# An adaLN + low-rank-expert FFN on one core: which DMA queue carries the first loads, and when the first stores leave

## The chip, the cores and the metric

The kernel runs on one NeuronCore of a Trainium2 chip. The metric is device microseconds (us) from launch to end; lower is better. Three runs of the kernel before the change took 791.09, 791.59 and 792.16 us, median 791.59. One further execution was recorded by the hardware profiler, and all durations below come from it.

Engines are called as in the profile: PE is TensorE (matmuls), PEld its weight loads, DVE is VectorE, ACT ScalarE, POOL GpSimd, SP SyncE. DMAs are issued in three places here: by SP (queue q1 of the profile), by ACT (q10), and by POOL (q0, software descriptors). All three feed the same 16 DMA engines.

## The reference

```
def cond(x, condition, weights):              # weights (16, 64, 64), one 64x64 matrix per sample
    return einsum('bct,bcd->bdt', x, weights[condition])
def ffn(y, A, B, Wr):                         # 64 experts of rank 16, top 16 of 64 per token
    scores = y @ Wr.T
    top_vals, top_idx = top_k(scores, 16)
    G = zeros(N, 64).at[rows, top_idx].set(softmax(top_vals))
    h = einsum('nd,krd->nkr', y, A)
    return einsum('nkr,kdr->nd', h * G[:, :, None], B) * 2.0
out = x + ffn(cond(x))                        # x is (64, 64, 1024) float32
```

So there are two 4096 x 1024 x 1024 products in float32, with the experts' gates multiplied in between, a small per-sample 64 x 64 product, and a residual add.

## The kernel before, in words

Tokens are handled in 8 groups of 512 rows. Each group has an "h" product (x with A) and an "o" product (the gated h with B). Both are done by Strassen-Winograd recursion: seven block products p1 to p7 instead of eight, built from sums and differences of blocks. For group 0 there is one level of it (functions z_whole and o_whole; matmuls at L542, tiles h_x, h_y, h_w, o_x, o_y, o_w). From group 1 on there are two levels (matmuls at L505). The second level needs sums of quarters of A and B ("leaves"). DVE makes these while group 0 is computed; leaf_steps makes them in a staging tile and stores them to HBM at L413 as h_p_p and o_p_p, and later parents fetch them from there (L458). Staging tiles come from the pool bsum, which has five buffers; the first four leaves use the tiles hb instead, which are still unused then. A sixth staging tile from bsum can only be written when the store out of the first has landed.

The schedule is written out by hand: the program order of each engine is the order in which the Python code calls it, and hooks (at(n, "mid" / "late" / "end", ...)) hang work for the other engines on the n-th parent product. Group 0 runs p1, p2, p5, p6, p7, p4, p3 of h. After p2 come the router scores of group 0, scores_t (L179, tile st), which need all four quarters of x and the router weight wr_sb. turn, scores, route_top, exps, rest, scaled and gates then turn these into gates; gates is a PE transpose (L301, tile gp) in the middle of p4, and gated (L321, tile zp) follows it.

What loads what at the start:

- ACT's queue: the first quarter of x in two parts, its three other quarters (L100, 512 KB each), and wr_sb (L118, 256 KB).
- SP's queue: a11 in two parts, a21, a12, a22 (L106, 1088 KB each), then the four blocks of B (L922, 1024 KB each).
- POOL's queue: cond_b (L110, the sample's condition broadcast to 128 partitions), the gathers of the 64 x 64 matrices (L157), six leaf stores of A's blocks a11 and a21 (L413), the residual rows of group 0 (L735, 512 KB each), later leaf stores.

A queue's DMAs are issued in order, and at most eight of those issued by SP and ACT together are in flight: where a ninth is due, its issuer waits for an earlier one to land, as the waits of SP's queue for DMAs of x show. Ten matmuls of the identity (L147, tile idle) run on PE ahead of the first product.

Of the kernel before, what the change touches and what calls it, by code (L numbers as in the profile page):

```python
# [15 lines left out]
P = 128  # L16
# [13 lines left out]
def kernel(  # L30
# [26 lines left out]
    nc = tc.nc  # L57
    N, T = x.shape
    B = cond.shape[1]
# [29 lines left out]
    def sub(o, a, b):  # L89
        nc.vector.tensor_tensor(o, a, b, ALU.subtract)  # L90
# [4 lines left out]
    def load_x(g: int, i: int, j: int, queue=nc.sync, parts=1):  # L95

        t = xq[g, i, j] = xp.tile([P, CH, HN], F32, tag=f"x{i}{j}", name=f"x_{g}_{i}{j}")
        for k in range(parts):
            s = ts(k, CH // parts)
            queue.dma_start(t[:, s, :], x_t[g, i, j][:, s, :])  # L100

    def load_block(name, src, r, c, pool, parts=1):
        t = pool.tile(src.shape[2:], F32, name=name)
        for k in range(parts):
            s = ts(k, CH // parts)
            nc.sync.dma_start(t[:, s, :], src[r, c][:, s, :])  # L106
        return t

    cond_b = const.tile([P, B], I32)
    nc.gpsimd.dma_start(cond_b, cond.to_broadcast([P, B]))  # L110
    load_x(0, 0, 0, nc.scalar, 2)
    a11 = load_block("a11", a_t, 0, 0, apool, 2)
    load_x(0, 1, 0, nc.scalar)
    a21 = load_block("a21", a_t, 1, 0, apool)
    load_x(0, 0, 1, nc.scalar)
    load_x(0, 1, 1, nc.scalar)
    wr_sb = epool.tile([P, 2 * CH, K], F32, name="wr_sb")
    nc.scalar.dma_start(wr_sb, wr_t)  # L118
    a12 = load_block("a12", a_t, 0, 1, apool)
    a22 = load_block("a22", a_t, 1, 1, apool)  # L120

# [19 lines left out]

    ident = const.tile([P, P], F32)
    make_identity(nc, ident)

    idle = acc.tile([P, P], F32, tag="acc", name="idle")
    for _ in range(10):
# [6 lines left out]
    def gather(g: int):  # L153
# [12 lines left out]
    hb = {  # L166
        (i, j): blocks.tile([P, CH, HN], F32, name=f"hb{i}{j}") for i in range(2) for j in range(2)
    }
# [171 lines left out]
    def left_sums(l):  # L340
        l11, l12, l21, l22 = l[0, 0], l[1, 0], l[0, 1], l[1, 1]
        ops = {"p1": l11, "p2": l12, "p4": l22}

        def tile_of(p):
            ops[p] = extra.tile([P, CH, HN], F32, tag="ex", name=f"sum_{p}")
            return ops[p]

        def s3():
            sub(l21, l11, l21)
            ops["p7"] = l21  # L350

        def s2():
            sub(tile_of("p6"), l22, ops["p7"])

        def s1():
            add(tile_of("p5"), ops["p6"], l11)

        def s4():
            sub(tile_of("p3"), l12, ops["p6"])

        def s1_s2():
            add(tile_of("p5"), l21, l22)
            sub(tile_of("p6"), ops["p5"], l11)

        return ops, {"s1": s1, "s2": s2, "s3": s3, "s4": s4, "s1_s2": s1_s2}
# [15 lines left out]
    def quads(t, w):  # L381

        return [[t[:, 2 * i : 2 * i + 2, ts(j, w)] for j in range(2)] for i in range(2)]

    leaf_d = {}
# [6 lines left out]
        (q11, _), (q21, q22) = quads(b_t[r, c], HALF)  # L392
        leaf_d.update({("o", j, "p1"): q11, ("o", j, "p2"): q21, ("o", j, "p3"): q22})

    unused = list(hb.values())

    def leaf_steps(k, j, block, apart=None):


        (q11, q12), (q21, q22) = quads(block, WIDTH[k])  # L400
        made = {}
        def staged(name):
            if apart is not None and unused:
                t = unused.pop().rearrange("p c k -> p (c k)")
                return t[:, : 2 * WIDTH[k]].rearrange("p (c k) -> p c k", c=2)
            t = bsum.tile([P, 2 * (HALF + KC)], F32, tag="leaf", name=name)
            return t[:, : 2 * WIDTH[k]].rearrange("p (c k) -> p c k", c=2)

        def step(op_, p, a, b):
            def f():  # L410
                made[p] = staged(f"{k}s_{j}_{p}")
                op_(made[p], *(made[v] if isinstance(v, str) else v for v in (a, b)))
                nc.gpsimd.dma_start(leaf_d[k, j, p], made[p])  # L413

            return f

        if k == "o":
            return [
                step(sub, "p5", q12, q11),
                step(sub, "p6", q22, "p5"),  # L420
                step(sub, "p4", q21, "p6"),
                step(sub, "p7", q22, q12),
            ]
        stay.update({(k, j, "p1"): q11, (k, j, "p2"): q21, (k, j, "p3"): q22, (k, j, "p5"): q12})
        t1 = q12 if apart is None else apart.rearrange("p (c k) -> p c k", c=2)
        steps = [
            step(sub, "p7", q22, q12),
            lambda: sub(t1, q12, q11),
            step(sub, "p6", q22, t1),
            step(sub, "p4", q21, "p6"),  # L430
        ]
        return steps if apart is None else steps + [lambda: nc.scalar.copy(q12, t1)]
# [416 lines left out]
    def x_operands(st):  # L849
        l = {(i, j): xq[st["g"], i, j] for i in range(2) for j in range(2)}  # L850
        st["x_ops"], st["x_sums"] = left_sums(l)
# [4 lines left out]
    def sums(st, which, *steps):  # L856
        for s in steps:
            st[which][s]()
# [61 lines left out]
    steps_of(first_steps["p2"], 4)  # L920
    for t, r, c in ((b12, 0, 1), (b22, 1, 1), (b11, 0, 0), (b21, 1, 0)):
        nc.sync.dma_start(t, b_t[r, c])  # L922
    x_operands(st)
    sums(st, "x_sums", "s1_s2")
    a_sums(1)
# [166 lines left out]
```

## Time and profile before

| what | value |
|---|---|
| runs | 791.09, 791.59, 792.16 us (median 791.59) |
| profiled execution, its own time | 791.37 us |
| its span, first to last instruction | 789.6 us |
| mean granted TensorE clock | 0.993 |
| PE busy | 772.7 us (98%) |
| DVE busy | 623.9 us (79%) |
| ACT, POOL busy | 184.7 us (23%), 76.5 us (10%) |
| DMA | 208.50 MB, mean 264 GB/s |

The profile page gives totals. The timeline lists instructions in order with, in brackets, the idle time before them and what ended it. The waits view sums such idle time by waiter and releaser. The windows view gives busy time, granted clock (PEclk) and DMA rate for chosen stretches. The DMA view lists queues and, for each issue, the size and the time to landing. Times are from the start of the span.

### The profile page before, as it was taken

The page shows a single profiled execution, that of the slowest core. Times are in us where ns is not written, and L with a number is a line of the kernel's source. Part 1 is how long each engine was busy: PE and PEld are TensorE (multiplying, and loading weights), DVE is VectorE, ACT ScalarE, POOL GpSimd, SP SyncE. Part 2 cuts the span into 40 slices and gives each one's busy share as a digit, 9 for nine tenths or more (in the row PEclk, how much of TensorE's full clock was granted, in tenths as well). Part 3 has the DMA queues.
Part 4 walks back from the last instruction along what each step waited for, and adds up shares of the span by engine and source line. Part 5 has one row for each costly group of instructions (what it writes and reads, how often), then busy time and mean ns, then how long its engine had stood idle before and what let it go on. Part 6 is the DMA issues. An engine that isn't in the chain of part 4 may idle for free.

```text
span 789.6 us, 14668 instructions
## 1 busy us (share of the span) xinstructions
PE 772.7 (98%) x5348; PEld 612.7 (78%) x5348; DVE 623.9 (79%) x1310; ACT 184.7 (23%) x490; POOL 76.5 (10%) x109
## 2 busy tenths in 40 slices
PE   8799999999999999999999999999999999999996
PEld 5344447888888888887888888888888888888885
DVE  3877875678788877898788977889768897688985
ACT  1031001223222322222223222232222231222221
POOL 4425353000010020000200001000200000000000
PEclk9899999999999999999999999999999999999999
DMA  9958569555778948887688968789488893687995
GB/s 327 410 214 287 193 245 307 184 186 161 279 244 284 349 129 323 270 294 263 217 291 280 307 213 278 264 279 339 140 309 275 277 352 121 220 267 250 343 384 209
DMA packets 107223, 208.50 MB, mean 264 GB/s; under 512 B 11072, under 2 KB 27200, under 8 KB 106256
## 3 DMA queue, kind: packets, MB, share of 16 engines
q1 hardware_dynamic: 99056, 183.33, 68.3%
q0 software_dynamic: 7088, 21.62, 7.8%
q10 hardware_dynamic: 1008, 2.62, 0.8%
q8 instruction: 43, 0.70, 0.3%
q14 instruction: 28, 0.23, 0.1%
HBM read 174.41 MB, written 33.11 MB: 263 GB/s over the span
## 4 chain that ended last, share of the span: by engine, by line
PE 93%; DMA 3%; DVE 2%; issue 0%; ACT 0%; DVEq 0%
PE h_p_x L505 23%; PE o_p_x L505 20%; PE h_p_w L505 12%; PE o_p_w L505 10%; PE h_p_y L505 6%; PE o_p_y L505 5%; PE zp L321 4%; PE o_x L542 4%; DMA wr_sb<-in_wr_t_dram 3%; PE h_x L542 3%; PE o_w L542 2%; PE h_w L542 2%; PE sw L221 1%; PE gp L301 1%; DVE o L87 1%; PE o_y L542 1%
## 5 line engine op out<-in xcount | busy, mean ns | idle before, releaser
L505 PE MATMUL o_p_x<-lo_p_p,l_t 128*128 128x256 f32 x584 | 142.9, 379 | 0.0
L505 PEld LDWEIGHTS o_p_x<-lo_p_p,l_t 128*128 128x128 f32 x584 | 111.0, 190 | 15.4
L87 DVE TENSOR_TENSOR o<-o,m_o_p 128x1024 f32<-128x1024 f32 (+1 forms) x67 | 78.8, 1195 | 0.5
L157 POOL DMA_INDIRECT w_st<-in_cw_dram,idx x32 | 34.0, 1061 | 431.2 <-PE zp L321 413.4
L87 DVE TENSOR_TENSOR m_h_p<-h_p_w,l_a 128x272 f32<-128x272 f32 x49 | 21.5, 440 | 62.5 <-PE h_p_w L505 62.5
L87 DVE TENSOR_TENSOR m_h_p<-m_h_p,m_h_p 128x1088 f32<-128x1088 f32 x49 | 62.3, 1283 | 0.2
L505 PE MATMUL h_p_x<-a,l_t 128*128 128x272 f32 x224 | 60.5, 392 | 0.0
L505 PE MATMUL h_p_w<-lh_p_p,l_t 128*128 128x272 f32 x196 | 53.8, 397 | 0.0
L505 PE MATMUL h_p_x<-lh_p_p,l_t 128*128 128x272 f32 x196 | 52.9, 392 | 0.0
L505 PE MATMUL o_p_w<-lo_p_p,l_t 128*128 128x256 f32 x196 | 51.1, 383 | 0.0
L334 DVE TENSOR_TENSOR hb<-zp,gg 128x512 f32<-128x512 f32 x64 | 39.9, 684 | 12.0 <-PE zp L321 12.0
L505 PEld LDWEIGHTS h_p_x<-a,l_t 128*128 128x128 f32 x224 | 42.6, 190 | 8.6
L598 ACT COPY l_b<-h_p_x 128x272 f32<-128x272 f32 x49 | 18.9, 386 | 121.8 <-PE h_p_x L505 119.5
L505 PE MATMUL h_p_x<-at,l_t 128*128 128x272 f32 x168 | 45.4, 392 | 0.0
L505 PEld LDWEIGHTS h_p_x<-lh_p_p,l_t 128*128 128x128 f32 x196 | 37.2, 190 | 7.5
L598 ACT COPY l_b<-o_p_x 128x256 f32<-128x256 f32 x49 | 18.2, 372 | 103.8 <-PE o_p_x L505 103.8
L505 PEld LDWEIGHTS h_p_w<-lh_p_p,l_t 128*128 128x128 f32 x196 | 36.5, 191 | 7.0
L505 PEld LDWEIGHTS o_p_w<-lo_p_p,l_t 128*128 128x128 f32 x196 | 36.6, 190 | 5.2
L87 DVE TENSOR_TENSOR m_o_p<-o_p_w,l_a 128x256 f32<-128x256 f32 x48 | 20.3, 423 | 23.2 <-PE o_p_w L505 23.2
L321 PEld LDWEIGHTS zp<-w_st,m_h_p 64*64 64x64 f32 x2048 | 31.7, 135 | 7.9 <-issue 7.9
L505 PEld LDWEIGHTS h_p_x<-at,l_t 128*128 128x128 f32 x168 | 31.9, 190 | 6.6
L605 ACT COPY m_h_p<-h_p_x 128x272 f32<-128x272 f32 x49 | 18.9, 387 | 70.7 <-PE h_p_x L505 70.7
(173 smaller groups left out, 1393.4 us busy)
## 6 DMA issues: line engine op xcount, KB each, us to landing
lo_p_p<-o_p_p SPq DMA_DIRECT2D x280, 256.0 KB, 3.7
lh_p_p<-h_p_p SPq DMA_DIRECT2D x147, 272.0 KB, 5.6
lo_p_p<-in_b_t_dram SPq DMA_DIRECT2D x63, 256.0 KB, 4.1
x<-in_x_t_dram SPq DMA_DIRECT2D x28, 512.0 KB, 5.5
o<-in_x_dram SPq DMA_DIRECT2D x28, 512.0 KB, 7.0
out_dram<-o SPq DMA_DIRECT2D x27, 512.0 KB, 4.4
o_p_p<-os_p_p POOLq DMA_DIRECT2D x28, 256.0 KB, 3.3
h_p_p<-hs_p_p POOLq DMA_DIRECT2D x17, 272.0 KB, 2.8
```

Of the source, the lines that this page charges most:

```text
L87: nc.vector.tensor_tensor(o, a, b, ALU.add)
L157: nc.gpsimd.indirect_dma_start(out=w_st[:, i, :], out_offset=None, in_=cw, in_offset=bass.IndirectOffsetOnAxis(ap=idx[:, n : n + 1], axis=0),)
L221: nc.tensor.matmul(sw[r, i, ts(k, K // 2)].rearrange("p (d k) -> p d k", d=2), lhsT=ws[g][r, i, :], rhs=halves(st["z"][i // 2, k])[r, i % ...
L301: nc.tensor.transpose(gp[:, i, :], st["g2"][i].rearrange("p a k -> p (a k)"), ident)
L321: nc.tensor.matmul(zp[b][e * D : (e + 1) * D, c, s, :], lhsT=halves(z)[r, s, c // 2, ds(c % 2 * P + e * D, D)], rhs=ws[g][r, 2 * i + s, :] ...
L334: nc.vector.tensor_tensor(tokens(hb[j, i])[:, :, :, b, :], zp[b], g_ij[:, :, :, b, :], ALU.mult)
L505: nc.tensor.matmul(bank, lhsT=v[:, c, :], rhs=w[:, c, :width], start=first and c == 0, stop=c == 1, skip_group_check=True,)
L542: nc.tensor.matmul(piles[n, s], lhsT=left()[j][:, c, ts(s, P)], rhs=w, start=c == 0 and PILES[kind][j].isupper(), stop=c == CH - 1, skip_g ...
L598: nc.scalar.copy(par["val"][n], par["bank"]["x"])
L605: nc.scalar.copy(before["q"][0][1], before["bank"]["x"])
```

## The change

The three other quarters of x and wr_sb go from ACT's queue to SP's, where they stand between the blocks of A in the order in which the program uses them. The load of cond_b on POOL moves behind the two POOL instructions that make the identity. The six stores of the first leaves (those of a11 and a21) go from POOL's queue to SP's, behind the four loads of B; their staging tiles stay occupied until those stores have landed. No computation changes.

```
     cond_b = const.tile([P, B], I32)
-    nc.gpsimd.dma_start(cond_b, cond.to_broadcast([P, B]))
     load_x(0, 0, 0, nc.scalar, 2)
     a11 = load_block("a11", a_t, 0, 0, apool, 2)
-    load_x(0, 1, 0, nc.scalar)
+    load_x(0, 1, 0)
     a21 = load_block("a21", a_t, 1, 0, apool)
-    load_x(0, 0, 1, nc.scalar)
-    load_x(0, 1, 1, nc.scalar)
+    load_x(0, 0, 1)
+    load_x(0, 1, 1)
     wr_sb = epool.tile([P, 2 * CH, K], F32, name="wr_sb")
-    nc.scalar.dma_start(wr_sb, wr_t)
+    nc.sync.dma_start(wr_sb, wr_t)
     a12 = load_block("a12", a_t, 0, 1, apool)
     a22 = load_block("a22", a_t, 1, 1, apool)
...
     ident = const.tile([P, P], F32)
     make_identity(nc, ident)
+    nc.gpsimd.dma_start(cond_b, cond.to_broadcast([P, B]))
...
-    unused = list(hb.values())
+    unused, to_store = list(hb.values()), []
...
                 op_(made[p], *(made[v] if isinstance(v, str) else v for v in (a, b)))
-                nc.gpsimd.dma_start(leaf_d[k, j, p], made[p])
+                if apart is None:
+                    nc.gpsimd.dma_start(leaf_d[k, j, p], made[p])
+                else:
+                    to_store.append((leaf_d[k, j, p], made[p]))
...
     for t, r, c in ((b12, 0, 1), (b22, 1, 1), (b11, 0, 0), (b21, 1, 0)):
         nc.sync.dma_start(t, b_t[r, c])
+    for d, t in to_store:
+        nc.sync.dma_start(d, t)
     x_operands(st)
```

## The prediction

> **What bounds the kernel now.** I read the page's totals first, then the waits of PE, then the windows and the timeline of the first 60 us, then the DMA view by stretches. PE is busy for 772.7 of 789.6 us, so only its idle time and slow-clock time can be won.
>
> ```profile
> PE 772.7 (98%) x5348; PEld 612.7 (78%) x5348; DVE 623.9 (79%) x1310; ACT 184.7 (23%) x490; POOL 76.5 (10%) x109
> ...
> PE st L179 <- DMA wr_sb<-in_wr_t_dram: 5.7, 1, 5.7
> PE idle L147 <- POOL ident masks.py:199: 2.8, 1, 2.8
> PE zp L321 <- issue: 0.3, 1, 0.3
> ```
>
> PE waits only twice: 2.8 us for the identity, and 5.7 us for wr_sb. From the second wait to the end it does not stop, so what PE gains up to 33 us reaches the end of the run unless a new wait eats it.
>
> ```profile
> 20.00:25.00 5.00, 1.42 (x4) 0.35 (x2) 2.02 (x2) 0.00 (x0) 3.31 (x4) 0.99 1.01 417
> 25.00:30.00 5.00, 2.83 (x14) 1.69 (x16) 4.97 (x3) 0.00 (x0) 2.76 (x2) 0.50 1.01 422
> 30.00:35.00 5.00, 5.00 (x25) 2.59 (x24) 4.96 (x6) 0.59 (x1) 1.46 (x2) 0.83 1.03 416
> ```
>
> Columns: window, length, busy PE, PEld, DVE, ACT, POOL, then clock, DMA share, GB/s. The wait costs twice: after it the clock is 0.50, then 0.83 on average. DMA is saturated at 417 to 422 GB/s and DVE is full from 25 us.
>
> ```profile
> q1 hardware_dynamic: 160, 1.16, 55.3%
> q0 software_dynamic: 168, 0.57, 28.1%
> q10 hardware_dynamic: 161, 0.35, 18.0%
> ```
>
> This is the DMA view of 20 to 25 us: packets, MB, share. SP's and ACT's queues alternate packet by packet (160 against 161), but SP's packets are larger, so x and wr_sb get 0.35 MB where A and B get 1.16. wr_sb lands at 27.1 though needed at 21.4.
>
> ```profile
> 27.17 5.89 PE st L179 x32
> ...
> 58.99 0.44 PE gp L301 x4
> ```
>
> These are two pieces of the chain that ended last (start, us): the scores that wait for wr_sb, and the transpose of the gates, the next place where PE depends on a long line of other engines' work.
>
> **The change part by part.**
>
> *Identity first.* POOL's iota and two identity instructions run from 2.09 to 2.76 behind the cond_b issue at 1.28; they move up by 0.8 us, and so does idle, which starts at 2.82 now. The first parts of x and a11 land at 5.4 and 5.2, before idle would end at 6.2. The next operands limit it: x's second quarter and a21 end, with all ahead of them, at 3.25 MB. Before, 3.27 MB had passed at 12.0 us (149, 258 and 411 GB/s in three windows of 4 us), and a21, with fewer bytes ahead of it, landed at 13.57; I take 13.5, so p2 starts near 13.5 instead of 14.0. Gain carried on: 0.8 at most, 0.5 to 0.8 with the 0.3 us wait of p2 gone.
>
> *wr_sb.* In the order of use it ends after 2.1 MB of x, 2.2 of a11 and a21 and 0.26: 4.6 MB, thus at 12.0 + 1.35/0.418 = 15.2, landing a microsecond later. PE wants it at 20.7. The 5.75 us go, and the clock loss with it. That loss: st took 5.89 us, of which it ran at half clock up to about 31.7 (0.50 to 30, and 0.83 over the next 5 us is about 1.7 us more at half), so (31.7 - 27.17)/2 = 2.3. **Sum up to here: 5.75 + 2.3 + 0.8 = 8.9 us**; PE would reach gp, at 58.99 now, at 50.1.
>
> Here a rule of the Trainium skill speaks against the change: "DMA: Bandwidth & Descriptors", section "Issuing engines are not separate DMA queues", says that all issuers share the same 16 engines and that another issuer only saves issue time. By that rule alone the move is worth 0. The trace agrees on the total (417 GB/s with three queues) but not on the conclusion: 160 against 161 packets of unequal size shows that the queue decides who lands first. I take the rows.
>
> *Cover of that gain.* p5 needs DVE's a_sums(1). cond_b is issued 0.8 later and lands at 10.5 (9.7 now; it took 8.4 from issue), DVE's idx follows, then four leaf steps (0.73 each) to 14.0, four more to 16.9, x sums 2.4 to 19.3, a_sums(1) 2.4 to 21.8. PE wants it at 24.2. Without the 6.5 us wait for x that DVE has now, it keeps ahead by 2.4 us. If cond_b came over 2.4 us later, each further us would be lost. ACT loses five DMA issues before its first copy at 13.7: nothing. Gathers: PE needs them at 32, they land about 22: nothing.
>
> *Six stores to SP, behind B.* On POOL six issues (3.3 us) go; its residual loads start near 21.5 to 24 instead of 28.6 to 33 and now share the DMA engines with B. They are not used before 84 us. On SP eleven issues of 0.35 to 0.4 us, about 4 us, are added, while SP is idle from 18.6 to 33.9; the next x quarter behind them is needed at 122.8. So issue is free. Landing is not. The fifth and sixth stores hold two of bsum's five tiles, and DVE's fourth leaf step of B (the sixth bsum tile) must wait for the fifth store.
>
> ```profile
> h_p_p<-hs_p_p POOLq DMA_DIRECT2D x1, 272.0 KB, 14.2
> ...
> 37.99 1.42 DVE L90 TENSOR_TENSOR os_p_p<-b,os_p_p 128x512 f32<-128x512 f32 x2
> 39.33 0.68 DVE L90 TENSOR_TENSOR os_p_p<-b 128x512 f32<-128x512 f32 x1
> 42.08 0.61 DVE L243 MAX8 tops<-sc 128x8 f32<-128x64 f32 x4 [2.07 <-ACT sc L229]
> ```
>
> Now the store issued at 18.1 lands at 32.3 and the step at 39.33 does not wait. After, DVE is at this step at 34.6: from 21.8, a_sums 2, 3, s3, the z add and a_sums 4 take it to 32.1 (21.8 + 2.5 + 2.4 + 1.2 + 1.3 + 2.4, and 0.5 for a22), three steps of 0.7 with the wait for b11 to 34.6. When does the store land? Ahead of its end: x, A, wr_sb, B 11.0 MB, five stores 1.4, gathers and cond_b 0.3, residual 1.6, and up to 0.8 of POOL's new leaf stores: 14.3 to 15.1 MB. From 3.27 MB at 12.0: 0.418 MB/us (mean of the 4 us windows to 32) gives 11.6 at 32; the rest at 0.393 (windows 32 to 40) ends at 38.8 to 40.9, and landing adds about 1.0. I take **41.0**. DVE stalls for 6.4 us.
>
> Behind this step in DVE's order stand route_top, five steps, rest, then ACT's scaled, and PE's gp waits for that. From the step's start to gp, by the rows: 0.7 (step) + 1.85 (tops, negs, sum_p) + 3.3 (five steps) + 5.1 (rest: 47.19 to 53.85 less the 1.54 wait) + 1.3 (scaled) + 0.25 for handovers = 12.5. gp comes at 53.5 instead of 50.1: **PE waits 3.4 us, and 8.9 - 3.4 = 5.5 is left.** After gp DVE is late by about a microsecond at most: the z add of p7 ends near 57.8, p3 needs it near 58.8; the sum for o's p7 ends about 73.8 and is wanted at 73.7. I take off 0.2. DVE waits on PE again (now 1.61 and 2.17 us before zp, 3.83 for a store at 114.95), so it catches up by 80 us. Net -5.3.
>
> Unknown costs. What a single hardware queue moves with these packets: the nearest row with SP's queue alone at full share is 300 to 305 us, 384 GB/s; the best here is 427. With 0.427 and 14.3 MB the store lands at 38.8 and 7.7 us are won; with 0.384 and 15.1 MB at 43.7, and 2.8. I stay between because the mix at 12 to 40 us is mostly the same loads. The clock at the new 3.4 us wait: the only idle PE in the trace, 5.75 us, cost 2.3. The Trainium skill, "TensorE: Matmul & The Clock Gate", section "Why this matters for your kernels", advises no PE gap above about 3 us, which would put 2 us more here; another part of the page calls the window 3.4 us and free-running. The granted clock here fell some 3.6 us after PE went idle (0.99 still in 20 to 25), so a 3.4 us gap seldom fills a window. I take 0; the end is +2.3.
>
> 791.4 - 5.3 = 786.1; the profiled execution is 0.2 below the median of the runs, so 786.3.
>
> **The rivals.**
>
> *The stall never reaches PE* (chance 0.2): the store lands by 38, or the waiting step finds another free tile. Then all 8.9 come: 782.5. For it: stores and loads may overlap better than the rows. Against it: five buffers, six tiles, and DMA saturated to 43 us now.
>
> *One queue is slow, and DVE's wait takes the place of PE's* (slower). gp is at 58.99 if the fifth store lands at 46.5, that is if the 11.8 MB behind 12.0 us move at less than 11.8/(46.5 - 1 - 12.0) = 0.352 MB/us. At 0.33 it lands at 48.8, gp comes 2.3 late and the long idle before it adds 2.3 of half clock: 791.6 + 4.6 = 796. For it: no stretch of the first 40 us has SP's queue alone. Against it: 384 at 300 us with smaller packets. Chance 0.07.
>
> *Half given back* (0.11): rate near 0.384, or a clock drop at gp: 787.5 to 790.
>
> *The order does nothing*, as wr_sb still lands late because SP waits for earlier landings before it issues. Against it: eight in flight keep over 3 MB queued, about 8 us of work, so such waits cost no bandwidth. 791.5, chance 0.04.
>
> **How the numbers follow.** The main case, 784 to 788, has 0.58. About 1.6 us (0.2%) can be told from no change. Faster: 0.58 + 0.2 + most of 0.11 = 0.88; same 0.05; slower 0.07. The range from 782.2 to 789.2 holds the main case, the full gain and most of the half-way case.
>
> **What would show it.** In the changed kernel: st follows h_y without a wait near 20.7 and takes 3.5 us at clock 1.00; a DVE wait of 4 to 8 us on os_p_p for the DMA h_p_p<-hs_p_p, ending near 41; a new PE wait at gp for ACT's g2 of 2 to 5 us. The prediction is wrong if gp waits for nothing, if PE waits for a_sums(1) before h_w, or if the DMA rate up to 35 us is under 380 GB/s.

## The result, and the profile after

The changed kernel took 786.55 us (median of four runs, 785.03 to 786.96), the kernel before 791.34 (median of four, 790.80 to 792.16). The ratio is 0.9935, with a 95% interval from 0.9918 to 0.9952: faster by 4.8 us (0.65%), where 5.3 were predicted. The profiled execution took 786.72 us (before 791.37), its span is 784.8 us, its mean clock 0.995. The traces below are of this execution.

First the row of totals from the page of the changed kernel, then the first rows of PE's waits (total us, times, longest).

```profile
PE 772.8 (98%) x5348; PEld 612.4 (78%) x5348; DVE 623.7 (79%) x1310; ACT 184.7 (24%) x490; POOL 74.3 (9%) x103
```

```profile
PE gp L301 <- ACT g L289: 2.7, 2, 2.6
PE idle L147 <- POOL ident masks.py:199: 1.5, 1, 1.5
PE zp L321 <- issue: 0.4, 1, 0.4
```

The work of the engines is what it was. The wait for wr_sb (5.7 us) is gone from the list, the wait for the identity is 1.5 instead of 2.8, and a new one of 2.6 us stands at gp. The next two fences show where the 5.7 us came from: the DMA view of the changed kernel for 4 to 9 us (issuer, KB, us from issue to landing), and the one for 20 to 25 us (packets, MB, share).

```profile
wr_sb<-in_wr_t_dram SPq DMA_DIRECT2D x1, 256.0 KB, 10.9
```

```profile
q1 hardware_dynamic: 262, 1.91, 95.7%
q0 software_dynamic: 106, 0.10, 5.9%
```

SP issues wr_sb at 5.51 and it lands at 16.4. Before, ACT issued it at nearly the same time, 5.44, and it landed at 27.1. In the window in which x's queue and A's had shared the packets evenly, 161 to 160, one queue now has a share of 95.7%. The total is no higher: 402 GB/s here, 417 before. Only the order has changed.

Now PE's timeline in the changed kernel (start, duration, engine, line, operation, tiles; in brackets the idle time before it and what ended it).

```profile
20.12 3.67 PE L179 MATMUL st<-x,wr_sb 128*64 128x256 f32 x32
...
39.26 10.46 PE L545 MATMUL h_x<-at,x 128*128 128x512 f32 x24
52.28 1.21 PE L301 MATMUL gp<-ident,g 128*128 128x128 f32 x4 [2.56 <-ACT g L289]
53.42 1.99 PE L321 MATMUL zp<-w_st,m_h_p 64*64 64x64 f32 x64
55.34 4.39 PE L545 MATMUL h_x<-at,x 128*128 128x512 f32 x8
...
66.43 3.60 PE L545 MATMUL o_x<-b,hb 128*128 128x512 f32 x8
```

And the same places in the kernel before:

```profile
58.83 0.60 PE L301 MATMUL gp<-ident,g 128*128 128x128 f32 x4
59.35 1.16 PE L321 MATMUL zp<-w_st,m_h_p 64*64 64x64 f32 x64
60.45 3.70 PE L542 MATMUL h_x<-at,x 128*128 128x512 f32 x8
...
70.85 3.60 PE L542 MATMUL o_x<-b,hb 128*128 128x512 f32 x8
```

The scores st start at 20.12 instead of 27.17 and take 3.67 us instead of 5.89. PE is ready for gp at 49.72 (52.28 less the idle 2.56), 9.1 us ahead of before. It then waits and is 6.55 ahead at gp. From gp to the first o_x it needs 14.15 us where before it needed 12.02, so it is 4.42 ahead at o_x, and stays so to the end (4.4). The windows view of the changed kernel says what those 2.1 us are (window, length, busy PE, PEld, DVE, ACT, POOL, clock, DMA share, GB/s):

```profile
50.00:51.00 1.00, 0.00 (x0) 0.00 (x0) 0.91 (x7) 0.00 (x0) 0.00 (x0) 1.00 0.88 356
51.00:52.00 1.00, 0.00 (x0) 0.00 (x0) 0.83 (x6) 0.17 (x1) 0.00 (x0) 1.00 0.07 29
...
53.00:54.00 1.00, 1.00 (x22) 0.72 (x26) 1.00 (x2) 1.00 (x3) 0.00 (x0) 0.68 0.00 0
54.00:55.00 1.00, 1.00 (x51) 1.00 (x48) 0.96 (x2) 0.11 (x1) 0.12 (x1) 0.50 0.00 0
55.00:56.00 1.00, 1.00 (x17) 0.71 (x11) 1.00 (x3) 0.00 (x0) 0.82 (x2) 0.50 0.08 25
56.00:58.00 2.00, 2.00 (x5) 0.87 (x4) 2.00 (x4) 0.00 (x0) 1.94 (x5) 0.81 0.86 318
```

After an idle time of 2.56 us the clock is 0.50 from about 53.4 to 56.8. zp takes 1.99 us instead of 1.16 and the eight matmuls of h_x take 4.39 instead of 3.70: 0.83 + 0.69 = 1.5 us. The other 0.6 is gp itself, 1.21 us instead of 0.60, since its four transposes now follow ACT's four pieces of g one by one.

Last, what makes gp late, in DVE's timeline of the changed kernel. The lines are B's second and third leaf, the fourth, and the first step of route_top.

```profile
33.91 1.42 DVE L90 TENSOR_TENSOR os_p_p<-b,os_p_p 128x512 f32<-128x512 f32 x2
40.36 0.69 DVE L90 TENSOR_TENSOR os_p_p<-b 128x512 f32<-128x512 f32 x1 [5.03 <-DMA o_p_p<-os_p_p]
40.97 0.60 DVE L243 MAX8 tops<-sc 128x8 f32<-128x64 f32 x4
```

The stall is at the predicted step and ends near the predicted time (41.0). But the store that ends it is o_p_p, one of B's own leaves on POOL's queue, not one of the moved h_p_p. The timelines of SP and of POOL and the DMA view for 33.5 to 34.4 us give the two candidates:

```profile
25.28 4.40 SPq L927 DMA_DIRECT2D h_p_p<-hs_p_p  x2
```

```profile
34.18 1.29 POOL L414 DMA_DIRECT2D o_p_p<-os_p_p  x2 [9.24 <-DVE os_p_p L90]
```

```profile
o_p_p<-os_p_p POOLq DMA_DIRECT2D x1, 256.0 KB, 6.2
```

The fifth moved store, issued at 25.28, takes 18.0 us (the same view for 23 to 26 us) and lands at 43.3, after the step has run. The store of B's first leaf, issued at 34.18, lands at 40.3, as the step starts. Each step waits for the semaphore (the counter that a DMA raises when it lands) of the store whose tile it takes, and the trace has these. In this kernel B's fourth and fifth step wait for the stores of B's first and second leaf, the sixth for the fifth moved store (landed 43.30, step at 43.53), the eighth for the sixth. So the tiles do not come round in order: the sixth tile asked of bsum, that of B's fourth leaf, is not the first one again. The DVE wait was there, but its owner was another than predicted, and how far the moved stores matter is what the first experiments ask.

### The profile page after: what moved, and what is told of

It is laid out like the page before. It is cut to its first block, busy times and chain, and to the rows that moved or that the text cites. A ratio compares the mean times of both kernels' runs of the same rounds, so it can differ in the third digit from the quotient of the medians.

```text
span 784.8 us, 14669 instructions
## 1 busy us (share of the span) xinstructions
PE 772.8 (98%) x5348; PEld 612.4 (78%) x5348; DVE 623.7 (79%) x1310; ACT 184.7 (24%) x490; POOL 74.3 (9%) x103
## 4 chain that ended last, share of the span: by engine, by line
PE 90%; DVE 3%; issue 3%; POOL 2%; DMA 2%; ACT 0%; POOLq 0%; DVEq 0%
PE h_p_x L508 23%; PE o_p_x L508 20%; PE h_p_w L508 12%; PE o_p_w L508 10%; PE h_p_y L508 6%; PE o_p_y L508 5%; PE zp L321 4%; PE o_x L545 4%; PE o_w L545 2%; POOL w_st L157 1%; PE gp L301 1%; DMA cond_b<-in_cond_dram 1%; DVE o L87 1%; PE sw L221 1%; PE o_y L545 1%
## 5 line engine op out<-in xcount | busy, mean ns | idle before, releaser
L334 DVE TENSOR_TENSOR hb<-zp,gg 128x512 f32<-128x512 f32 x64 | 39.9, 683 | 9.8 <-PE zp L321 9.8
```

Source lines behind the costliest of these rows:

```text
L334: nc.vector.tensor_tensor(tokens(hb[j, i])[:, :, :, b, :], zp[b], g_ij[:, :, :, b, :], ALU.mult)
```

## The experiments

Each is compared with the kernel before on the same chip; the experiments ran on three chips, so between them the ratios compare better than the times. Theory A is that of the prediction: the moved stores hold the staging tiles and so set gp. Its rival is that the stores of B's own leaves do.

### The six stores back on POOL's queue, the rest of the change kept

```
-                if apart is None:
-                    nc.gpsimd.dma_start(leaf_d[k, j, p], made[p])
-                else:
-                    to_store.append((leaf_d[k, j, p], made[p]))
+                nc.gpsimd.dma_start(leaf_d[k, j, p], made[p])
```

> The changed kernel with one part undone: the six first leaves' stores are back on POOL's queue, where they were; loads and identity stay as changed. Theory A (the moved stores make DVE's fourth leaf step of B wait, and so the gates late): that step, at 40.4 us after a 5.0 us wait in the changed kernel, comes near 37 with a wait under 1 us, gp (52.3 after a 2.6 us wait) comes near 49.7 with no wait, the clock does not fall there, and the time is about 5 us below the changed kernel, 781 to 783. Theory B (the wait is for a store of DVE's own new leaf, o_p_p, and the DMA engines are full to 41 us in any order, B landing later where the stores go first): the step waits as long for one thing or another, gp waits 2 to 3 us, 785.5 to 787.

Measured: 788.10 us, ratio 0.9953 [0.9936, 0.9969]. DVE's timeline, fourth and sixth leaf step of B:

```profile
36.45 0.69 DVE L90 TENSOR_TENSOR os_p_p<-b 128x512 f32<-128x512 f32 x1
...
43.58 0.69 DVE L90 TENSOR_TENSOR os_p_p<-b,os_p_p 128x512 f32<-128x512 f32 x1 [4.00 <-DMA o_p_p<-os_p_p]
```

The fourth step runs at once, since the two staging tiles of A's leaves are free early. But then the sixth step has no tile, for the same kind of reason: the store of B's first leaf, now issued at 35.37 on a fuller POOL queue, has not landed before 43.5. gp comes at 52.96 after a wait of 2.96 us, no earlier than in the changed kernel, and here too the granted clock falls to 0.50 afterwards, from 54.6 to 58.0 us. The time is above what either theory said. Theory A falls as it stands: with the moved stores gone from SP the gap at gp stays. What they change here is which step waits: with two tiles held to 43.3 and 44.0 there are three left, and the fourth step waits; with five tiles two steps more can run, and the sixth waits. In both kernels a step ahead of rest needs the store of B's first leaf. The moved stores come back into it below, where the residual loads are out of the way.

### Each part of the change alone

The stores alone (the kernel before, with `to_store` and its loop behind the loads of B):

> The kernel before with only the stores moved to SP behind B. Theory A: DVE reaches the fourth leaf step of B at 39.3 here, the stores land near 40 to 42, so it waits 1 to 3 us, most of which its later idle time (2.1 us before tops, 1.5 before es, 1.5 before gp) takes up: 791 to 792. Theory B: no wait there at all, 791.3. With six stores fewer ahead of them the SP and ACT loads share with less, so wr_sb may land up to 2 us earlier, 789.5 to 791.

Measured: 790.66 us, ratio 0.9986 [0.9979, 0.9993]. PE's waits, and DVE's fourth leaf step:

```profile
PE st L179 <- DMA wr_sb<-in_wr_t_dram: 5.2, 1, 5.2
```

```profile
41.19 0.69 DVE L90 TENSOR_TENSOR os_p_p<-b 128x512 f32<-128x512 f32 x1 [2.05 <-DMA h_p_p<-hs_p_p]
```

Here the step does wait for a moved store, as predicted of the whole change. It costs nothing, because PE comes to gp late enough: DVE waits 2.07 us for ACT's scores ahead of tops in the kernel before, and the new wait takes the place of that one. The kernel is even 0.9 us faster (the interval leaves out 1), since with six stores fewer in the way wr_sb lands at 26.2 instead of 27.1.

The identity alone (the kernel before, with the load of cond_b behind make_identity):

> The kernel before with only the load of cond_b moved behind the identity. PE starts idle and p1 about 1.2 us earlier, then waits for x's second quarter at 14.0 and for wr_sb at 27.1 as before: 791.3, no difference (both theories). A rival: if cond_b's packets, which hold the DMA engines at about 60 GB/s near 6 to 7 us, hurt less later, loads land up to 0.5 us earlier: 790.8.

Measured: 791.25 us, ratio 0.9995 [0.9989, 1.0002], no difference. PE's waits:

```profile
PE st L179 <- DMA wr_sb<-in_wr_t_dram: 5.8, 1, 5.8
PE idle L147 <- POOL ident masks.py:199: 1.5, 1, 1.5
PE h_x L542 <- DMA x<-in_x_t_dram: 0.8, 1, 0.8
```

PE starts 1.3 us earlier and waits for x, and then for wr_sb, until nearly the same time as before (26.71, before 27.17). By themselves these two parts bring 0.9 us and nothing, so the order of the loads carries the gain. That order alone, with neither of the other parts, was not run, nor was a move of wr_sb alone.

### The loads in order without the identity's move

```
     cond_b = const.tile([P, B], I32)
+    nc.gpsimd.dma_start(cond_b, cond.to_broadcast([P, B]))
...
     make_identity(nc, ident)
-    nc.gpsimd.dma_start(cond_b, cond.to_broadcast([P, B]))
```

> The changed kernel with the load of cond_b back ahead of the identity; loads and stores stay as changed. PE reaches gp 1.0 to 1.3 us later (50.8 in place of 49.7), but gp is set by DVE's chain behind the staging tile, near 52.3, so it comes when it came: 786.5, and since the idle stretch shrinks to about 1.5 us the clock may stay up, which would even bring 1.7 us: 784.8 to 786.6. If the identity's place is worth its 1.3 us: 787.8.

Measured: 786.17 us, ratio 0.9939 [0.9915, 0.9963], the same as the whole change. PE's timeline:

```profile
52.28 1.21 PE L301 MATMUL gp<-ident,g 128*128 128x128 f32 x4 [0.99 <-ACT g L289]
```

gp is at 52.28 to the hundredth as in the changed kernel, while PE waits 1.6 us less for it: what PE does earlier, it waits longer here, so the line through DVE sets gp. And after the shorter gap the profiled execution shows no drop: the clock stays at 1.00 and o_x comes at 64.92, 12.6 us after gp. Its four runs took 784.49 and 784.79 at mean clocks of 0.998 and 0.997, and 788.38 and 787.55 at 0.995. The runs with the higher clock are some 3 us faster. A drop like that in the changed kernel's trace would explain half of that; no slower run of this kernel was profiled, so the rest is open.

### Filling the gap at gp

Twenty, and in another kernel ten, matmuls of the identity ahead of gp; their output is overwritten by the transposes.

```
+        if not st["g"]:
+            for _ in range(20):        # 10 in the second kernel
+                nc.tensor.matmul(gp[:, 0, :], lhsT=ident, rhs=ident, start=True, stop=True)
```

> The changed kernel with 20 matmuls of the identity put on PE just ahead of the gate transposes of group 0, into the same PSUM tile that the transposes then overwrite; they fill PE's 2.6 us wait for ACT's scaled gates. If the clock drop after that wait (0.50 for 3.4 us) costs its 1.7 us, the clock stays at 1.00 and the time falls by 1.5 to 2 us, to about 784.8. If the drop costs nothing, or comes from something else, 786.5.

Measured with twenty: 788.64 us, ratio 0.9966 [0.9955, 0.9978]: slower than the changed kernel, where a gain of 1.5 to 2 us or nothing was expected. The filler takes 4.63 us, from 49.61 to 54.24, longer than the gap. gp comes at 54.08 at full clock and o_x at 66.10, only 0.3 us earlier than in the changed kernel. PE is 4.75 us ahead of before up to 200 us, but only 2.2 us ahead at the end. The losses, 1.5 and 1.7 us, are at two PE waits which the trace gives no releaser (0.6 us comes back between, where the kernel before has such a wait):

```profile
PE zp L324 <- issue: 2.6, 2, 1.4
```

One ends at 202.70 us, one at 739.03. The traces have a lead that no experiment tested: queue q8 (kind "instruction") makes 43 loads of 16 KB in a run, and two of them begin at 200.35 and 736.52, 2.4 and 2.5 us before these waits end. The 12 PE waits without a releaser of over 0.25 us in all the traces, all in zp, end 2.2 to 2.6 us after such a load began; in the kernel before it is one of 0.31 us at 370.89, with the load at 368.59. Matmuls that are added at 50 us may shift where in the program these loads fall. That they cause the waits is not shown. With ten:

> The changed kernel with 10 identity matmuls ahead of the gate transposes, half of the earlier filling run, whose filler (4.5 us) was longer than the gap (2.6 us) and which lost 1.5 us in the middle and 1.7 us at the end in zp matmuls that waited for nothing the profile shows. Here the filler takes 2.2 us. If the clock drop costs what the first run says (from gp's start to the first o_x: 12.0 us with the clock at 1.00, 14.3 without), the first o_x starts near 64.4 in place of 66.6, and 784.5 is reached if the added instructions cost nothing later; if they cost again 1.5 to 3 us there, 786 to 787.5.

Measured: 785.24 us, ratio 0.9917 [0.9900, 0.9934]. PE's timeline (each matmul of the identity has two records):

```profile
49.61 2.39 PE L302 MATMUL gp<-ident 128*128 128x128 f32 x20
52.21 1.21 PE L304 MATMUL gp<-ident,g 128*128 128x128 f32 x4 [0.20 <-ACT g L289]
53.34 1.16 PE L324 MATMUL zp<-w_st,m_h_p 64*64 64x64 f32 x64
54.44 3.70 PE L548 MATMUL h_x<-at,x 128*128 128x512 f32 x8
...
64.84 3.60 PE L548 MATMUL o_x<-b,hb 128*128 128x512 f32 x8
```

This prices the clock by itself. gp is where it was, zp and h_x have their old durations, and gp to o_x takes 12.63 us instead of 14.15: the drop costs 1.5 us. The pacing by ACT stays (gp 1.21). Of the 1.6 us won at o_x, 1.0 is lost again at one wait without a releaser, which ends at 735.80, and 0.6 comes back near 366 us, where the kernels before and after the change have such a wait and this one has none. The median is 1.3 us below the changed kernel's, and the two intervals overlap: the total of this kernel does not prove it, the durations in the trace do.

### What holds B's first leaf store

In the changed kernel the residual rows of group 0 stand ahead of the leaf stores of B on POOL, and they share the DMA engines with them. One kernel loads them three products later.

```
-            at(h + 2, "mid", load_res, st, (0, 0), (1, 1), (1, 0))
+            at(h + 5, "mid", load_res, st, (0, 0), (1, 1), (1, 0))
```

> The changed kernel with the residual loads of group 0 (three of 512 KB on POOL's queue, issued at 22.7 to 25 us) hung on p4 instead of p5, about 50 us. The run with the stores back on POOL still waited 4 us at a leaf step of B for an o_p_p store and still had gp 3.0 us late, so theory A in its first form is gone. Theory B (DVE waits for a staging tile whose own store stands behind the 1.5 MB of residual loads in POOL's queue, with the DMA engines full to 43 us): without these loads the store issued at 34.2 lands by 38 instead of 40.4, DVE's wait falls from 5.0 to 2.5 us or less, gp waits under 0.5 us, the clock stays, and PE keeps its 9.2 us: 782 to 783. Theory C (SP's B and leaf stores alone keep the engines full past 40 us): the store lands within 0.5 us of where it did, 786.5.

Measured: 785.36 us, ratio 0.9926 [0.9910, 0.9943].

```profile
39.14 0.69 DVE L90 TENSOR_TENSOR os_p_p<-b 128x512 f32<-128x512 f32 x1 [4.66 <-DMA o_p_p<-os_p_p]
...
69.09 0.72 DVE L90 TENSOR_TENSOR hs_p_p<-at,hs_p_p 128x544 f32<-128x544 f32 x1 [2.91 <-DMA h_p_p<-hs_p_p]
```

The store still takes about 5.8 us from its issue, so the residual loads alone do not make it long, and the step is only 1.2 us earlier. gp comes at 50.68 after a wait of 0.72, with no drop of the clock. But the loads now stand ahead of later leaf stores; DVE waits 2.91 us for one of them, and a new wait reaches PE:

```profile
PE o_w L545 <- DVE hb L90: 1.4, 1, 1.4
```

The same with the stores back on POOL:

> The changed kernel with the six stores back on POOL and the residual loads late as well. It tells whether the moved stores matter once the residual loads are out of the way. Theory B: POOL's own leaf stores then have no backlog ahead but the six, which land by 33; no wait at gp, 782 to 783, as with the stores on SP. If the six stores on POOL delay B's blocks (b11 came 1.2 us later in that run), DVE starts B's steps a microsecond later, which the slack at gp still takes up.

Measured: 783.60 us, ratio 0.9898 [0.9881, 0.9914]. No leaf step of B waits, gp runs at 49.65 without a gap, and PE waits 0.9 us at o_w. At o_x it is 9.2 us ahead of before (61.68). Of that, 1.0 us goes at o_w and 2.0 more by the end, part of it a wait for an o_p_p leaf of 1.0 us at 748.18.

Four kernels now differ in these two things alone: where the six stores are, and when the residual loads come. In each cell stand the median, how long the store of B's first leaf took from issue to landing, and the gap at gp (us):

| residual loads | six stores on SP | six stores on POOL |
|---|---|---|
| at p5, early | 786.55; 6.2; 2.56 | 788.10; 8.1; 2.96 |
| at p4, late | 785.36; 5.8; 0.72 | 783.60; 3.8; none |

With neither in the way, the store issued at 35.85 lands at 39.67, by its semaphore's updates in the trace. With either one alone it takes 5.8 us or more, so taking one away at a time does not show it. Loading the residual rows later removes most of the gap (2.56 to 0.72), and moving the stores back removes the rest, though the two intervals of that pair still touch. Whether that last step comes from the shorter landing, from the two tiles that are free earlier, or from the store's being issued 2.5 us later, these runs do not separate.

### The waiting leaf step behind the top-k

If the fourth leaf step blocks DVE ahead of route_top, it can stand behind it.

```
-        (h + 2, b_steps, 4),
+        (h + 2, b_steps, 3),
         (h + 3, b_steps, 5),
-        (h + 4, b_steps, 3),
+        (h + 4, b_steps, 4),
```

> The changed kernel with one leaf step of B (the fourth, which waits 5.0 us ahead of route_top) moved behind route_top and the sum of x: 3 steps at p5, 5 at p7's predecessor as before, 4 instead of 3 after rest. Nothing else differs. If what is queued behind the wait is what costs (DVE's order), tops come near 36 instead of 41 and rest starts near 44.6 instead of 46.5, since the wait now stands behind fewer steps; gp comes 1.9 us earlier, the gap is under 1 us and the clock stays: 782.5 to 784. If rest's start is set by the last free tile and not by the order, the gain is under 0.7 us.

Measured: 783.17 us, ratio 0.9896 [0.9878, 0.9914]. DVE's and PE's timelines:

```profile
34.04 0.60 DVE L243 MAX8 tops<-sc 128x8 f32<-128x64 f32 x4
...
39.90 0.69 DVE L90 TENSOR_TENSOR os_p_p<-b 128x512 f32<-128x512 f32 x1 [3.93 <-DMA o_p_p<-os_p_p]
```

```profile
50.81 1.21 PE L301 MATMUL gp<-ident,g 128*128 128x128 f32 x4 [0.84 <-ACT g L289]
```

The store lands at nearly the same time (39.9, before 40.3), but tops (40.97 in the changed kernel) and the sum of x are done ahead of the wait, so their durations lie in the stall. rest starts 1.45 us earlier (45.02 against 46.47), the gap at gp is 0.84 us, the clock stays at 1.00, and o_x comes at 63.44. Now that DVE is earlier, the predicted wait comes up too: the sixth leaf step of B waits for the fifth moved store.

```profile
43.09 1.42 DVE L90 TENSOR_TENSOR os_p_p<-b,os_p_p 128x512 f32<-128x512 f32 x2 [1.47 <-DMA h_p_p<-hs_p_p]
```

No later PE wait takes the gain back: the intervals of this kernel and of the changed one do not overlap.

One more step moved (3, 4, 5):

> The changed kernel with two leaf steps of B moved later (3 steps at p5, 4 after the sum of x, 5 after rest, in place of 4, 5 and 3). With one moved, rest started at 45.0 and gp still waited 0.8 us. If DVE's order ahead of rest is what sets gp, rest starts 0.7 us earlier, gp waits under 0.3 us, and the time is 0.5 to 0.8 us below that run: 782.4 to 783. If DVE is late further on (the sum that o's p7 needs), a PE wait at o_w appears and nothing is won: 783 to 784.5.

Measured: 782.92 us, ratio 0.9887 [0.9871, 0.9904], the fastest of all, though not to be told from the one above. rest starts at 44.69, only 0.3 us earlier, since DVE again waits for the fifth moved store (1.20 us).

```profile
50.25 1.21 PE L301 MATMUL gp<-ident,g 128*128 128x128 f32 x4 [0.64 <-ACT g L289]
...
62.89 3.60 PE L545 MATMUL o_x<-b,hb 128*128 128x512 f32 x8
```

The later residual loads and the fourth step moved, together:

> Both edits together on the changed kernel. If each alone removes gp's wait, both together bring nothing beyond the 9.2 us that PE has at gp without it: 782. If each alone removes a part, the sum of both, but not below 782.

Measured: 784.03 us, ratio 0.9910 [0.9886, 0.9935]. gp runs at 50.01 with no gap, but PE waits 1.8 us at o_w for DVE, which waits 2.56 us for an h_p_p store: the later loads again. The two gains do not add, and the 782 expected is missed by 2 us.

### A sixth place for a leaf

The fourth leaf of B is staged in gg, a tile that is not yet in use then.

```
+            if name == "os_p1_p7":
+                return gg.rearrange("p (c k) -> p c k", c=2)
```

> The changed kernel with the fourth leaf of B staged in the tile gg, which is unused until the gates are written, in place of one from bsum: one staging tile more, order and queues unchanged. If DVE's 5.0 us wait is for a staging tile, the fourth step runs without a wait at 35.3, tops come at 36, and the wait moves to the fifth step, to about 40.4; rest starts near 44.6, gp waits 0.5 to 1 us and the clock stays: 783 to 784, like the run with one step moved. If the step waits for something else, 786.5.

Measured: 784.34 us, ratio 0.9910 [0.9894, 0.9927].

```profile
34.16 0.68 DVE L90 TENSOR_TENSOR gg<-b 128x512 f32<-128x512 f32 x1
...
40.13 0.69 DVE L90 TENSOR_TENSOR os_p_p<-b 128x512 f32<-128x512 f32 x1 [3.44 <-DMA o_p_p<-os_p_p]
```

The fourth step runs at once, and the fifth meets the same store at the same time. This shows that the wait is one for a staging tile: one more tile moves it by one step. tops runs at 34.76, gp at 51.58 after 1.62 us, more than the 0.5 to 1 expected, as DVE then waits 2.01 us for the fifth moved store at 43.95. The clock stays at 1.00.

## Why the prediction was right, point by point

**The loads in order: right.** wr_sb was to land a microsecond after 15.2 and landed at 16.4. st was to follow h_y near 20.7 in 3.5 us and did so at 20.12 in 3.67. PE was to be ready for gp at 50.1 and was at 49.7. The rows of packets decided this, not the rule that the prediction set against them: the total rate did not rise, and the order was worth the gain.

**Identity first: size off, worth as said or less.** idle moved up by 1.3 us, not 0.8, as POOL's own start was 0.4 us earlier too. Alone it gave nothing, and leaving it out of the change gave nothing measurable either, since gp does not move with it.

**cond_b later: harmless, as said, for another reason.** It was to land 0.8 us later. It was issued at 1.54 instead of 1.28 and took 8.0 us instead of 8.4, so it landed at 9.5, no later than before. The cover held: a_sums(1) ended at 21.85 (21.8 was said) and h_w followed at 23.72.

**The DVE wait: right step, wrong store, and the time by luck.** The step "must wait for the fifth store" failed. The step took the tile of B's first leaf and waited for that leaf's store, which the prediction did not consider because it did not stall anything before. The sum went wrong at the order of the tiles: it took the sixth tile to be the first one again, and in the kernel with the stores alone that is so, but not in this one. The fifth store landed at 43.3 rather than 41.0; by then the engines had moved 16.0 MB (369 GB/s over 43.3 us), where the sum had 14.3 to 15.1. That another store ended the wait at 40.3 is luck. Had the step waited to 43.3, gp would have come near 55.2 by the measured 11.9 us from step to gp (an estimate), a gap of 5.5 us. The moved stores are not without effect: they hold two tiles, with them on SP and the residual loads late the store of B's first leaf takes 5.8 us instead of 3.8, and DVE does wait for one of them in the kernels that are ahead of this one.

**gp and the gap: a little better than said.** From step to gp 11.9 us instead of 12.5, gp at 52.28 instead of 53.5, a gap of 2.56 instead of 3.4.

**The clock: the term that was mis-sized.** "I take 0" was wrong in this execution: the drop cost 1.5 us. The prediction argued that a 3.4 us gap seldom fills a window; gaps of 2.56 us here and of 2.96 with the stores on POOL were enough. In the five traces with a drop ahead of the end it begins 3.4 to 5.2 us after PE went idle and lasts 3.4 or 6.8 us, so the 3.6 us read from the kernel before is no fixed delay. Three of four runs of the changed kernel have the low mean clock of 0.995 (786.4 to 787.0 us) and one has 0.997 (785.0). The Trainium skill's advice of "TensorE: Matmul & The Clock Gate", section "Why this matters for your kernels", to stay under about 3 us, would have priced it for the gap predicted, and it too is above the gaps that did it. Besides, gp's pacing by ACT, 0.6 us, was not in the sum.

**The sum.** Predicted -8.9 + 3.4 + 0.2 = -5.3. Measured: 9.1 us ahead on reaching gp, 2.56 lost there, then 1.5 and 0.6: -9.1 + 2.56 + 2.1 = -4.4 at o_x, -4.65 in the profiled times. The shorter gap made up for half of what the clock took, so the closeness of the total is in part luck.

**The rivals.** A slow single queue is excluded: 399 to 414 GB/s in the windows of 4 us from 12 to 40 us. That the order does nothing is excluded by st. That the stall never reaches PE was not this kernel, but it is within reach of it: the two kernels with leaf steps moved come to 783.17 and 782.92, near the 782.5 worked out for it. Of "half given back" the one cause, a clock drop at gp, did come; the total stayed under 787.5 because the gap was shorter than said.

**Left open.** By what rule a leaf gets its tile, since the fourth step of B takes an h_p_p tile in the kernel with the stores alone and an o_p_p tile in the changed one; why a clock drop comes in some executions of a kernel and not in others; and what takes back 1 to 2 us behind 731 us in three of the kernels (both fillers, and the one with the late loads and the stores on POOL).

## What to carry to other kernels

In these traces queues that are busy at the same time share the engines by packets (160 to 161), so an urgent load of small packets beside a queue of large ones arrived late; in one queue in the order of use it arrived 10.7 us earlier at no higher total rate. When the last load wait of an engine goes, look for the next thing that this engine needs from a long line of others, and for every buffer in that line that is released by a store: the stores that never stalled before are candidates too. In an engine's program order, put the step that may wait for a buffer behind the steps that others wait for.

## What was not expected of the hardware

- An idle time of 2.56 us on PE halved the granted clock for 3.4 us, beginning about 1 us after PE was back at work. It cost 1.5 us. A gap of 2.96 us in another kernel did the same; gaps of 0.64 to 1.62 us in five other traces did not, and the mean clocks suggest that it comes in some executions of a kernel and not in others.
- Twenty small matmuls put into that gap saved the clock, but two waits of PE without a releaser followed much later and took 3.2 us; with ten, one took 1.0 us. That the filler brings them is not shown; such waits end 2.2 to 2.6 us after a 16 KB instruction load on q8 began, and the kernel before has one too.
- The store of a 256 KB leaf took 3.8 us from issue to landing with neither the moved stores nor the residual loads in the way, and 5.8 to 8.1 us with either or both.
- The load of cond_b on POOL's queue took about 8 us whether it was issued at 1.28 or at 1.54 us.
